# A prefix state in a causal linear-attention block: one fp32 product per chunk replaced by three fp32r products over halves, with the values stored twice

## The chip, the cores and the metric

The kernel runs on one NeuronCore of a Trainium2 chip. The metric is the device time of one execution in microseconds, taken as the median of several runs. The core's engines are named as in the profile: PE is TensorE's matmul, PEld its weight load, DVE is VectorE, ACT is ScalarE, POOL is GpSimd, and SP is SyncE, whose queue issues all of this kernel's DMA transfers.

## The reference

4096 tokens of width 512 go through a linear-attention layer with 16 query heads and 4 key/value heads of width 128, a layer norm, a gated feed-forward layer with Hadamard transforms, and another layer norm. The change lies in the attention, which is, for every head:

```python
q = q * cos + _rotate_half(q) * sin
k = k * cos + _rotate_half(k) * sin
qf = jax.nn.elu(q) + 1.0
kf = jax.nn.elu(k) + 1.0
def step(carry, inp):
    state, z = carry
    state = state + k_s[..., :, None] * v_s[..., None, :]
    z = z + k_s
    num = jnp.einsum('bhe,bhed->bhd', q_s, state)
    den = jnp.einsum('bhe,bhe->bh', q_s, z)[..., None] + EPS
    return ((state, z), num / den)
```

So a state of 128 by 128 (the sum of the outer products of k and v over all tokens so far) is carried along the sequence, and each token's query is multiplied with it.

## The kernel before

**Tiling.** The tokens are cut into 16 blocks of 256 (NB), each block into four chunks of 64. Two of the four key/value heads are done at a time: the loop `for i, (n, g, p) in enumerate(slots)` runs over n = 0 to 31 (the pass s = n // 16 over the head pair, the block b = n % 16), the head g of the pair and the half p of the block (two chunks). So a block has four slots, (0,0), (0,1), (1,0), (1,1), and there are 128 slots. In the first pass x is split into high and low halves and written to HBM (`xs_d`), in the second the halves are read back.

**Halves.** Most products are made in fp32r from operands that are split as hi = round(x) and lo = x - hi (`hilo`, L95 and L96): hi*hi + hi*lo + lo*hi, three matmuls accumulated in PSUM. The projections (`proj_v` L241, `proj` L288) are made so.

**What one block does.** `proj_v` makes v (ps_v, 128 tokens by 2 by 256), copies it in fp32 (v32, L245), makes its halves (vhl, high at L247 by ACT, low at L249 by DVE, each multiplied by rowm_s, which is zero at rows 0 and 64) and sends two sets of DMA copies from SBUF to SBUF: vd (each chunk's 64 rows stored twice, in partitions 0 to 63 and 64 to 127, four copies of 256 KB) and vs (v shifted by 63 rows, so that it lines up with the running sum that leads into a chunk, three copies). `rope` applies the rotary factors and elu + 1 (L268 to L278, over ACT, POOL and DVE). `proj_k` makes k (kft, transposed, L306 to L316 make its halves khl and the running sum z). `nat_k` transposes k back (pt, L325) and copies it to SBUF in fp32 (kfn, L327).

`state` adds a block's part to the running state for one head: four fp32 products of kfn and vs (L337), one per chunk, those of the even chunks over 64 rows and those of the odd chunks over 128:

```python
for i in range(4):
    r = slice(0, 64 * (i % 2) + 64)
    T.matmul(ps[:, i], B["kfn"][r, g, i // 2], B["vs"][r, i // 2, g * 128:(g + 1) * 128],
             start=True, stop=True)
```

Then DVE adds the state that came before (L348), ACT makes the high half sh (L353) and DVE the low half sl (L355). `scores` multiplies q with k inside a chunk (L380, L381), ACT and DVE fold the halves (L387, L390, L391) and POOL masks the result (A, L394). `av` adds state times q (sh and sl with qh and ql, three matmuls) and A times vd (two matmuls, L414), and the denominator (L415); ACT copies the result (num, L418), which goes to HBM by DMA.

**What sets the order.** The slot loop writes the calls in an order by hand: in slot (0,0) the state of block n for head 1, in (0,1) `proj_v` and `load_x` of later blocks, in (1,0) `nat_k` of block n + 1, in (1,1) the state of block n + 1 for head 0. Generators (`go`) split each call into pieces that are spread over a slot. q is projected five slots ahead (QA), the scores one (SA). Within that, a planner in the tile framework orders the instructions of each engine and of SP's queue by a simulated timeline; only those that the program pins (`pin`) keep their place. All DMAs go through SP, in order: a DMA that waits holds up those behind it.

**Buffers.** vs, vhl and kfn have one buffer, vd two, x1 three, num three, ds two; ps_s and pt share one PSUM bank (pst).

After the last slot come the output projection, layer norm, feed-forward stage and its output, which the change leaves as they are.

Of the kernel before, what the change touches and what calls it, by code (L numbers as in the profile page):

```python
# [9 lines left out]
F32 = mybir.dt.float32  # L10
# [33 lines left out]
def kernel(  # L44
# [3 lines left out]
    cs, ident, had, sel, rowm, out,  # L48
# [30 lines left out]
    rowm_s = cpool.tile([128, 1], F32, name="rowm_s")  # L79
# [8 lines left out]
    def load_raw(src):  # L88
        pool, tag = first.pop(0) if first else (praw, "raw")
        raw = pool.tile([128, 512], F32, tag=tag, name="raw")  # L90
        dma(raw, src)
        return raw
# [86 lines left out]
    with ExitStack() as es:  # L179
# [14 lines left out]
        G.memset(neg1, -1.0)  # L194
        W = {}
# [36 lines left out]
        def proj_v(n):  # L232
# [11 lines left out]
            v32 = pe.tile([128, 2, 256], F32, tag="v32", name="v32")  # L244
            S.activation(v32, ps, AF.Copy)  # L245
            vhl = p1.tile([128, 2, 2, 256], F32R, tag="vhl", name="vhl")
            S.activation(vhl[:, 0], ps, AF.Copy, scale=rowm_s)  # L247
            yield
            V.scalar_tensor_tensor(vhl[:, 1], ps, rowm_s, vhl[:, 0].bitcast(F32), ALU.mult, ALU.subtract)  # L249
            vd = p2.tile([128, 2, 4, 256], F32R, tag="vd", name="vd")  # L250
            for half in range(2):
                for par in range(2):
                    dst = vd[half * 64:half * 64 + 64].rearrange("p l (t r) d -> p l t r d", r=2)[:, :, :, par]
                    dma(dst, vhl[par * 64:par * 64 + 64])
            vs = p1.tile([128, 2, 256], F32, tag="vs", name="vs")
            dma(vs[63:128], v32[0:65])
            dma(vs[0:63, 1], v32[65:128, 0])
            if b:
                dma(vs[0:63, 0], blk[n - 1]["v32"][65:128, 1])
            else:  # L260
                G.memset(vs[0:63, 0], 0.0)
            B.update(v32=v32, vd=vd, vs=vs)

        def rope(ps, csb, f, stay=False):
# [8 lines left out]
            x1 = ps if stay else pe.tile([128, 2, 256], F32, tag="x1", name="x1", bufs=3)  # L273
# [45 lines left out]
        def nat_k(n):  # L319
# [6 lines left out]
            kfn = p1.tile([128, 2, 2, 128], F32, tag="kfn", name="kfn")  # L326
            S.activation(kfn, pt, AF.Copy)  # L327
            B["kfn"] = kfn
            B["S"] = []

        def state(n, g):
# [3 lines left out]
            for i in range(4):  # L335
                r = slice(0, 64 * (i % 2) + 64)
                T.matmul(ps[:, i], B["kfn"][r, g, i // 2], B["vs"][r, i // 2, g * 128:(g + 1) * 128],  # L337
                         start=True, stop=True)
# [16 lines left out]
            V.tensor_tensor(sl, s32, sh.bitcast(F32), ALU.subtract)  # L355
# [41 lines left out]
        def av(n, g, p):  # L397
# [10 lines left out]
            for c2 in range(2):  # L408
# [3 lines left out]
                       (B["vd"][:, 0, c, gs], A[:, c2]), (B["vd"][:, 1, c, gs], A[:, c2])]  # L412
# [4 lines left out]
            num = p3.tile([128, 4, 2, 64], F32, tag="num", name="num")  # L417
# [3 lines left out]
            if p == 1:  # L421
                ds = pout.tile([4, 256], F32, tag="ds", name="ds", bufs=2)
# [53 lines left out]
        first.extend([(praw, "raw")] * 3 + [(p3, t) for t in ("num", "s32", "sh", "sl") for _ in range(3)])  # L476
# [7 lines left out]
        dma(rowm_s, rowm)  # L484
# [27 lines left out]
        run(proj_v(0))  # L512
        weights_q(0, 0)
# [4 lines left out]
        nat_k(0)  # L518
# [15 lines left out]
        for i, (n, g, p) in enumerate(slots):  # L534
# [18 lines left out]
            if sl == (0, 0):  # L553
# [6 lines left out]
                gs2 = state(n, 1)  # L560
                go(gs2)
# [666 lines left out]
def _layout(inp):  # L1228
# [24 lines left out]
    for _ in range(7):  # L1253
# [3 lines left out]
    r = np.ones((128, 1), f)  # L1257
    r[0] = r[64] = 0
    arr["rowm"] = r
# [4 lines left out]
          "cs", "ident", "had", "sel", "rowm"]  # L1264
# [18 lines left out]
```

## Time and profile before

| what | value |
|---|---|
| median of 3 runs | 2303.36 us (2300.53 to 2303.75) |
| the profiled execution's own time | 2299.27 us |
| its span in the profile | 2297.6 us |
| attention stage (last state call) | from 0 to about 920 us |
| state products (L337), records and busy | 512, 112.3 us |
| mean granted PE clock | 0.994 |
| DMA, 50 to 900 us | 139.11 MB, mean 164 GB/s |

The page of a profile gives first the busy time of each engine. A busy time is the union of the records' lengths, and the matmuls' lengths overlap, since they are pipelined; the distance from one start to the next tells what one costs. A group of instructions is written as line, engine, operation, output and inputs, shapes, count. In the waits, what stands behind the arrow is what ended the wait. The timelines list start and length in us from the start of the span; merged lines have a count.

### The profile page before, as it was taken

What the parts mean: (1) busy time and instruction counts of PE and PEld (TensorE: products, weight loads), DVE (VectorE), ACT (ScalarE), POOL (GpSimd) and SP (SyncE); (2) the same over time, 40 slices, a digit from 0 to 9 for tenths busy, and PEclk for the clock granted to TensorE, in tenths of its full rate; (3) what the DMA queues carried; (4) which work ended last, traced back from release to release, by engine and by line L of the source; (5) the groups of instructions that cost most, each with busy time, mean ns of one, the idle gap of its engine ahead of it and who ended that gap; (6) DMA issues with size and microseconds to landing.
All of it is one profiled execution on the core that took longest, in us unless ns stands there. A gap on an engine that the chain in (4) does not pass through costs nothing. (4 is left out here: it accounts for less than half of the span.)

```text
span 2297.6 us, 42221 instructions
## 1 busy us (share of the span) xinstructions
PE 2258.7 (98%) x14432; PEld 2004.3 (87%) x14432; DVE 1757.2 (76%) x2684; ACT 1393.8 (61%) x2515; POOL 1280.1 (56%) x1063
## 2 busy tenths in 40 slices
PE   8999999999999999899999999999999999999998
PEld 7999999899999998688878878878788888899998
DVE  8888888888888878688898775766766766675555
ACT  7777777777777767444443466665555655464553
POOL 5556666555555545568797535665555555633332
PEclk9999999999999999999999999999999999999999
DMA  6665665555555544889998976876765757887773
GB/s 195 176 181 167 184 181 171 168 156 150 167 165 154 170 135 142 301 271 277 284 285 258 309 252 214 253 239 190 230 208 186 242 185 211 260 276 238 227 251 121
DMA packets 369527, 484.15 MB, mean 211 GB/s; under 512 B 68670, under 2 KB 224384, under 8 KB 365344
## 3 DMA queue, kind: packets, MB, share of 16 engines
q1 hardware_dynamic: 369312, 481.45, 68.4%
q8 instruction: 114, 1.87, 0.3%
q14 instruction: 101, 0.83, 0.1%
HBM read 282.76 MB, written 156.76 MB: 191 GB/s over the span
## 5 line engine op out<-in xcount | busy, mean ns | idle before, releaser
L288 PE MATMUL ps_qk<-xh,wh 128*128 128x256 f32 x1280 | 355.3, 278 | 0.0
L288 PE MATMUL ps_qk<-xl,wh 128*128 128x256 f32 x1280 | 354.9, 277 | 0.0
L288 PE MATMUL ps_qk<-xh,wl 128*128 128x256 f32 x1280 | 354.4, 277 | 0.0
L394 POOL TENSOR_SCALAR_AFFINE_SELECT A<-A 64x512 fp32r<-64x512 f32 x256 | 211.5, 826 | 241.8 <-DVE am L390 145.0
L1027 POOL TENSOR_TENSOR cc<-cc 128x512 f32<-128x512 f32 x96 | 149.0, 1554 | 288.8 <-ACT cc L1024 109.7
L96 DVE TENSOR_TENSOR wol<-A,woh 128x512 fp32r<-128x512 f32 x217 | 223.3, 1036 | 104.4 <-ACT woh L95 92.7
L270 POOL TENSOR_TENSOR sw<-sw,csb 128x512 f32<-128x512 f32 x160 | 208.5, 1303 | 135.2 <-ACT sw L269 124.2
L288 PEld LDWEIGHTS ps_qk<-xh,wh 128*128 128x128 f32 x1280 | 240.7, 188 | 3.0
L288 PEld LDWEIGHTS ps_qk<-xh,wl 128*128 128x128 f32 x1280 | 240.4, 188 | 0.9
L288 PEld LDWEIGHTS ps_qk<-xl,wh 128*128 128x128 f32 x1280 | 240.6, 188 | 0.3
L95 ACT ACTIVATE woh<-A 128x512 fp32r<-128x512 f32 x217 | 135.5, 630 | 134.6 <-PE ps_b L1045 76.5
L95 ACT ACTIVATE hah<-hraw 128x512 fp32r<-128x512 f32 x216 | 133.7, 629 | 125.5 <-PE ps_da L1196 63.8
L96 POOL TENSOR_TENSOR hal<-hraw,hah 128x512 fp32r<-128x512 f32 x78 | 106.9, 1374 | 175.2 <-PE ps_da L1196 75.0
L1045 PE MATMUL ps_a<-yoh,woh 128*128 128x512 f32 x512 | 202.6, 397 | 1.2 <-ACT sv L1052 1.0
L1045 PE MATMUL ps_a<-yol,woh 128*128 128x512 f32 x512 | 202.4, 395 | 0.0
L1045 PE MATMUL ps_a<-yoh,wol 128*128 128x512 f32 x512 | 199.8, 396 | 0.0
L96 DVE TENSOR_TENSOR hal<-hraw,hah 128x512 fp32r<-128x512 f32 x138 | 108.7, 796 | 98.0 <-PE ps_da L1196 40.0
L1052 ACT ACTIVATE sv<-ps_a,wsc 128x512 f32<-128x512 f32 x192 | 127.0, 680 | 38.1 <-PE ps_a L1045 37.8
L173 PE MATMUL ps_wo<-wh,oh 128*128 128x512 f32 x372 | 147.8, 397 | 2.1 <-ACT oh L95 2.1
L173 PE MATMUL ps_wo<-wh,ol 128*128 128x512 f32 x372 | 147.6, 397 | 0.0
L173 PE MATMUL ps_wo<-wl,oh 128*128 128x512 f32 x372 | 147.3, 396 | 0.0
L271 DVE TENSOR_TENSOR ps_qk<-ps_qk,csb 128x512 f32<-128x512 f32 x160 | 111.2, 695 | 32.6 <-ACT sw L269 30.9
(280 smaller groups left out, 7356.4 us busy)
## 6 DMA issues: line engine op xcount, KB each, us to landing
hraw<-hop_d SPq DMA_DIRECT2D x224, 256.0 KB
vd<-vhl SPq DMA_DIRECT2D x128, 256.0 KB
num_d<-num SPq DMA_DIRECT2D x128, 256.0 KB
rb<-rec_d SPq DMA_DIRECT2D x128, 256.0 KB
hop_d<-hS SPq DMA_DIRECT2D x128, 256.0 KB
nt<-num_d SPq DMA_DIRECT2D x31, 1024.0 KB
A<-in_wug_dram SPq DMA_DIRECT2D x93, 256.0 KB
hop_d<-cc SPq DMA_DIRECT2D x64, 256.0 KB
```

What stands on the lines that cost most here:

```text
L95: i = S.activation(hi, src, AF.Copy)
L96: j = eng.tensor_tensor(lo, src, hi.bitcast(F32), ALU.subtract)
L173: T.matmul(ps, l[:, h], r, start=i == 0, stop=i == 47)
L270: G.tensor_tensor(sw, sw, sinb, ALU.mult)
L271: V.tensor_tensor(ps, ps, cosb, ALU.mult)
L288: T.matmul(ps[:, j], W[key][wa][:, k * 128:(k + 1) * 128], B[xa][:, k], start=i == 0, stop=i == 11)
L394: G.affine_select(ah, ah.bitcast(F32), pattern=[[0, 8], [1, 64]], compare_op=ALU.is_ge, fill=0.0, base=0, channel_multiplier=-1)
L1027: G.tensor_tensor(x, x, c.pop(("g", q)), ALU.mult)
L1045: T.matmul(ps, w[:, u, k], y[:, k], start=first and i == 0, stop=i == 5, skip_group_check=not first)
L1052: S.activation(x, ps, AF.Copy, scale=sc)
```

## The change

The state's products are made in fp32r from halves. k's transposed-back copy is split into high and low (kfn gets a dimension of two, the low half by DVE from PSUM). v's copy for the state, vst, holds both halves, and holds v for both chunks of a pair side by side in 256 columns: the even chunk's columns are zero in partitions 64 to 127, so that both chunks take the same 128 rows of k, and one product serves two chunks. Per call that is two pairs times three products of 256 columns. The zeros are written once, as vst has one buffer; the fp32 copy v32 is gone. The last 63 rows of a block's halves are kept in vcar for the next block. The halves lie side by side in vhl, vst and vd, so that the copies have rows of 2 KB, and vst's copies are issued ahead of vd's. vd becomes two fixed tiles VD whose rows 0 and 64 are zeroed once, and its copies leave out these rows (63 rows in place of 64); rowm, which zeroed them, is gone with its input and its load. The low half of the state of head 1 goes to GpSimd. x1, num and ds lose a buffer each. `nat_k` becomes a generator, and the very last `state` call moves from slot (0,0) of the last block to slot (1,1) of the block before.

Left out of the diff are only the lines that take away rowm's tile, input and load.

```diff
@@ -86,8 +85,8 @@
         tc.keep_in_program_order(i)
 
     def load_raw(src):
-        pool, tag = first.pop(0) if first else (praw, "raw")
-        raw = pool.tile([128, 512], F32, tag=tag, name="raw")
+        pool, tag, nb = first.pop(0) if first else (praw, "raw", 3)
+        raw = pool.tile([128, 512], F32, tag=tag, name="raw", bufs=nb)
         dma(raw, src)
         return raw
@@ -192,6 +191,22 @@
         G.memset(ones4, 1.0)
         neg1 = p1.tile([128, 1], F32, name="neg1")
         G.memset(neg1, -1.0)
+        vst = pe.tile([128, 2, 2, 2, 256], F32R, name="vst", bufs=1)
+        vcar = pe.tile([128, 2, 256], F32R, name="vcar", bufs=1)
+        VD = [p2.tile([128, 4, 2, 256], F32R, tag="vd", name="vd") for _ in range(2)]
+
+        def zero(eng, dst):
+            src = ones4[0:dst.shape[0], 0:1, None].to_broadcast(list(dst.shape))
+            if eng is S:
+                S.activation(dst, src, AF.Copy, scale=0.0)
+            else:
+                V.tensor_scalar(dst, src, 0.0, None, ALU.mult)
+
+        for l in range(2):
+            for k in range(2):
+                zero(S if k else V, VD[k][:, 2 * l:2 * l + 2].rearrange("p c l d -> p (c l) d"))
+            zero(V, vst[64:128, l, 0])
+            zero(S, vst[0:64, 0, l])
         W = {}
         blk = {}
@@ -241,25 +256,28 @@
                         T.matmul(ps[:, t], B[xa][:, k, t * 128:(t + 1) * 128], w[:, k % 2],
                                  start=i == 0, stop=i == 11)
                         i += 1
-            v32 = pe.tile([128, 2, 256], F32, tag="v32", name="v32")
-            S.activation(v32, ps, AF.Copy)
-            vhl = p1.tile([128, 2, 2, 256], F32R, tag="vhl", name="vhl")
-            S.activation(vhl[:, 0], ps, AF.Copy, scale=rowm_s)
-            yield
-            V.scalar_tensor_tensor(vhl[:, 1], ps, rowm_s, vhl[:, 0].bitcast(F32), ALU.mult, ALU.subtract)
-            vd = p2.tile([128, 2, 4, 256], F32R, tag="vd", name="vd")
+            vhl = pe.tile([128, 2, 2, 256], F32R, tag="vhl", name="vhl", bufs=1)
+            S.activation(vhl[:, :, 0], ps, AF.Copy)
+            yield
+            V.tensor_tensor(vhl[:, :, 1], ps, vhl[:, :, 0].bitcast(F32), ALU.subtract)
+            dma(vst[63:128, :, 1], vhl[0:65])
+            dma(vst[63:64, :, 0], vhl[0:1])
+            dma(vst[0:63, 1], vhl[65:128, 0, None].to_broadcast([63, 2, 2, 256]))
+            if b:
+                dma(vst[0:63, 0], vcar[0:63, None].to_broadcast([63, 2, 2, 256]))
+            vd = VD[n % 2]
             for half in range(2):
                 for par in range(2):
-                    dst = vd[half * 64:half * 64 + 64].rearrange("p l (t r) d -> p l t r d", r=2)[:, :, :, par]
-                    dma(dst, vhl[par * 64:par * 64 + 64])
-            vs = p1.tile([128, 2, 256], F32, tag="vs", name="vs")
-            dma(vs[63:128], v32[0:65])
-            dma(vs[0:63, 1], v32[65:128, 0])
-            if b:
-                dma(vs[0:63, 0], blk[n - 1]["v32"][65:128, 1])
-            else:
-                G.memset(vs[0:63, 0], 0.0)
-            B.update(v32=v32, vd=vd, vs=vs)
+                    dst = vd[half * 64 + 1:half * 64 + 64].rearrange("p (t r) l d -> p t r l d", r=2)[:, :, par]
+                    dma(dst, vhl[par * 64 + 1:par * 64 + 64])
+            if b == 0 and n:
+                zero(V, vst[0:63, 0, 0])
+                zero(V, vst[0:63, 0, 1])
+            B.update(vhl=vhl, vd=vd)
+
+        def carry(n):
+            if n < N and n % NB < NB - 1:
+                dma(vcar[0:63], blk[n]["vhl"][65:128, 1])
 
         def rope(ps, csb, f, stay=False):
             cosb = csb[:, 0:1].to_broadcast([128, 2, 256])
@@ -270,7 +288,7 @@
             G.tensor_tensor(sw, sw, sinb, ALU.mult)
             V.tensor_tensor(ps, ps, cosb, ALU.mult)
             yield
-            x1 = ps if stay else pe.tile([128, 2, 256], F32, tag="x1", name="x1", bufs=3)
+            x1 = ps if stay else pe.tile([128, 2, 256], F32, tag="x1", name="x1", bufs=2)
             V.scalar_tensor_tensor(x1, ps, 1.0, sw, ALU.add, ALU.add)
             S.activation(sw, x1, AF.Exp, bias=neg1)
             yield
@@ -323,19 +341,21 @@
             for g in range(2):
                 for j in range(2):
                     T.transpose(pt[:, g, j], kft[:, g, 1 + 128 * j:129 + 128 * j], idt)
-            kfn = p1.tile([128, 2, 2, 128], F32, tag="kfn", name="kfn")
-            S.activation(kfn, pt, AF.Copy)
+            kfn = pe.tile([128, 2, 2, 2, 128], F32R, tag="kfn", name="kfn", bufs=1)
+            S.activation(kfn[:, 0], pt, AF.Copy)
             B["kfn"] = kfn
             B["S"] = []
+            yield
+            V.tensor_tensor(kfn[:, 1], pt, kfn[:, 0].bitcast(F32), ALU.subtract)
 
         def state(n, g):
             s, b = divmod(n, NB)
             B = blk[n]
             ps = pst.tile([128, 4, 128], F32, tag="st", name="ps_s")
-            for i in range(4):
-                r = slice(0, 64 * (i % 2) + 64)
-                T.matmul(ps[:, i], B["kfn"][r, g, i // 2], B["vs"][r, i // 2, g * 128:(g + 1) * 128],
-                         start=True, stop=True)
+            for j in range(2):
+                for i, (k, v) in enumerate(((0, 0), (0, 1), (1, 0))):
+                    T.matmul(ps[:, 2 * j:2 * j + 2], B["kfn"][:, k, g, j], vst[:, j, :, v, g * 128:(g + 1) * 128],
+                             start=i == 0, stop=i == 2)
             s32 = p3.tile([128, 4, 128], F32, tag="s32", name="s32")
             for i in (0, 2):
                 if i:
@@ -352,7 +372,7 @@
             yield
             S.activation(sh, s32, AF.Copy)
             yield
-            V.tensor_tensor(sl, s32, sh.bitcast(F32), ALU.subtract)
+            (G if g else V).tensor_tensor(sl, s32, sh.bitcast(F32), ALU.subtract)
 
         def proj_q(j):
             n, g, hp = j // 4, j // 2 % 2, j % 2
@@ -409,17 +429,17 @@
                 c = 2 * p + c2
                 t = slice(64 * c, 64 * c + 64)
                 ops = [(sh[:, c], qh[:, :, t]), (sh[:, c], ql[:, :, t]), (sl[:, c], qh[:, :, t]),
-                       (B["vd"][:, 0, c, gs], A[:, c2]), (B["vd"][:, 1, c, gs], A[:, c2])]
+                       (B["vd"][:, c, 0, gs], A[:, c2]), (B["vd"][:, c, 1, gs], A[:, c2])]
                 for i, (l, r) in enumerate(ops):
                     T.matmul(ps[:, c2], l, r, start=i == 0, stop=i == len(ops) - 1)
                 T.matmul(den, selr[:, c], A[:, c2], start=c == 0, stop=c == 3)
             gg = 2 * s + g
-            num = p3.tile([128, 4, 2, 64], F32, tag="num", name="num")
+            num = p3.tile([128, 4, 2, 64], F32, tag="num", name="num", bufs=2)
             S.activation(num.rearrange("p h c q -> p c h q"),
                          ps.rearrange("p c (h q) -> p c h q", h=4), AF.Copy)
             dma(num_d[2 * b + p][:, gg], num.rearrange("p h c q -> p (h c q)"))
             if p == 1:
-                ds = pout.tile([4, 256], F32, tag="ds", name="ds", bufs=2)
+                ds = pout.tile([4, 256], F32, tag="ds", name="ds", bufs=1)
                 S.activation(ds, den, AF.Copy, bias=EPS_DEN)
                 for j in range(2):
                     dma(den_d[2 * b + j][gg].rearrange("h c q -> c h q"),
@@ -473,7 +493,7 @@
         N = 2 * NB
         slots = [(n, g, p) for n in range(N) for g in range(2) for p in range(2)]
         NQ = len(slots)
-        first.extend([(praw, "raw")] * 3 + [(p3, t) for t in ("num", "s32", "sh", "sl") for _ in range(3)])
+        first.extend([(praw, "raw", 3)] * 3 + [(p3, "num", 2)] * 2 + [(p3, t, 3) for t in ("s32", "sh", "sl") for _ in range(3)])
 
         def early_raw(key, src):
             RAW0[key] = load_raw(src)
@@ -510,12 +529,13 @@
                 pass
 
         run(proj_v(0))
+        carry(0)
         weights_q(0, 0)
         run(proj_k(0))
         run(proj_q(0))
         weights_q(0, 1)
         run(proj_q(1))
-        nat_k(0)
+        run(nat_k(0))
         run(load_x(1))
         for j in range(2):
             c = slice(j * 512, (j + 1) * 512)
@@ -557,8 +577,9 @@
                     gv = proj_v(n + 1)
                     go(gv)
                 go(gs1)
-                gs2 = state(n, 1)
-                go(gs2)
+                if nxt:
+                    gs2 = state(n, 1)
+                    go(gs2)
             elif sl == (0, 1):
                 if n < N - 2:
                     gv = proj_v(n + 1)
@@ -568,7 +589,9 @@
                     run(load_x(n + 2))
             elif sl == (1, 0):
                 if nxt:
-                    nat_k(n + 1)
+                    gn = nat_k(n + 1)
+                    go(gn)
+                    carry(n + 1)
             else:
                 gs1 = state(n + 1, 0) if nxt else None
                 go(gs1)
@@ -585,8 +608,14 @@
                     go(gv)
             elif sl == (0, 1):
                 go(gv)
+            elif sl == (1, 0):
+                if nxt:
+                    go(gn)
             elif sl == (1, 1):
                 go(gs1)
+                if n == N - 2:
+                    gs2 = state(N - 1, 1)
+                    go(gs2)
             av(n, g, p)
             if sl == (0, 0):
                 go(gs2)
```

More of the change, by code (lines that the diff above doesn't have):

```diff
@@ L47 @@
     x_t, x_n, wq, wk, wv, wo, su_ug, su_dp, ws_ug, ws_dp, wug, wd,
-    cs, ident, had, sel, rowm, out,
+    cs, ident, had, sel, out,
 ):
@@ L78 @@
     idt = cpool.tile([128, 128], F32, name="idt")
-    rowm_s = cpool.tile([128, 1], F32, name="rowm_s")
     selr = cpool.tile([128, 4, 4], F32R, name="selr")
@@ L483 @@
             early_raw(("v", 0, j), wv[0, :, j * 512:(j + 1) * 512])
-        dma(rowm_s, rowm)
         for j in range(2):
@@ L1256, in _layout @@
     arr["sel"] = c(np.tile(np.eye(4, dtype=f).reshape(1, 16), (128, 1)))
-    r = np.ones((128, 1), f)
-    r[0] = r[64] = 0
-    arr["rowm"] = r
     return arr
 _ORDER = ["x_t", "x_n", "wq", "wk", "wv", "wo", "su_ug", "su_dp", "ws_ug", "ws_dp", "wug", "wd",
-          "cs", "ident", "had", "sel", "rowm"]
+          "cs", "ident", "had", "sel"]
 def kernel(**inputs):
```

## The prediction

> **What bounds the kernel now.** I read the page first, then a table by stretch, then the engines' timelines within one block, then the waits. The page names the engine:
>
> ```profile
> span 2297.6 us, 42221 instructions
> PE 2258.7 (98%) x14432; PEld 2004.3 (87%) x14432; DVE 1757.2 (76%) x2684; ACT 1393.8 (61%) x2515; POOL 1280.1 (56%) x1063
> PEclk9999999999999999999999999999999999999999
> ```
>
> TensorE is busy 98% of the span at full clock. The change touches only the first stage, about 0 to 922 us, so I cut two pairs of blocks out of it, one from the first pass over the blocks (s=0) and one from the second (s=1). Columns: stretch, its length, busy us and instructions of PE, PEld, DVE, ACT, POOL, clock, DMA share, GB/s.
>
> ```profile
> 316.80:344.30 27.50, 27.50 (x225) 26.06 (x224) 24.59 (x40) 20.74 (x40) 15.63 (x16) 1.00 0.65 192
> 344.30:372.90 28.60, 28.60 (x234) 27.13 (x233) 25.55 (x40) 21.39 (x40) 17.81 (x18) 1.00 0.58 167
> 544.50:572.50 28.00, 28.00 (x229) 26.55 (x229) 23.82 (x40) 20.39 (x38) 14.86 (x16) 1.00 0.56 152
> 572.50:600.50 28.00, 28.00 (x229) 26.59 (x228) 24.07 (x39) 19.87 (x37) 14.28 (x15) 1.00 0.62 177
> ```
>
> A block takes 28.0 us in both passes and PE is never idle in it. So what PE is spared comes off the span until another engine is late. VectorE is next: 25.1 of 28.05 us in the first pass, 23.95 of 28.0 in the second. The waits agree: between 50 and 880 us PE's matmuls waited for others 5.5 us in all (four rows), and not once for the state's operands.
>
> The work that changes, in PE's timeline (start, length, line, shape, count):
>
> ```profile
> 400.93 0.28 PE L288 MATMUL ps_qk<-xh,wh 128*128 128x256 f32 x1
> 401.05 0.28 PE L288 MATMUL ps_qk<-xl,wh 128*128 128x256 f32 x1
> 401.26 1.74 PE L337 MATMUL ps_s<-vs,kfn 64*128 64x128 f32 x8
> 402.75 0.36 PE L288 MATMUL ps_qk<-xh,wl 128*128 128x256 f32 x1
> ...
> 405.19 0.28 PE L414 MATMUL ps_num<-qh,sh 128*128 128x256 f32 x1
> 405.31 0.28 PE L414 MATMUL ps_num<-ql,sh 128*128 128x256 f32 x1
> 405.43 0.28 PE L414 MATMUL ps_num<-qh,sl 128*128 128x256 f32 x1
> ```
>
> The lengths overlap; the cost is the distance of starts. A 256-column fp32r product costs 0.12 us. The eight records of one state call (four fp32 products, two records each) hold PE from 401.05 to 402.75, 1.70 us, of which 0.12 is the matmul before: 1.58 us.
>
> **The products.** Removed: 64 calls x 1.58 = 101 us. Added: 64 calls x 6 products of 128x128 weights and 256 columns, whose nearest row is L414's qh,sh: 6 x 0.12 = 0.72, 46 us. Net 0.86 per call, 1.72 per block, 55 us. A block's floor on PE is 28.0 - 1.72 = 26.3 us.
>
> Here a rule speaks against the change. The Trainium skill, "FP8 and Floating Point Precision", section TensorE Precision Notes, gives true fp32 four passes through the array. A pass of 128 columns at the rate of the row above is 0.06 us, so four passes are 0.24 per product and 0.94 per call; against 0.72 the change would spare 0.22 per call, 14 us. The trace has 1.58, almost twice that, so I take the trace; the 14 us are a rival's number.
>
> **VectorE, ScalarE, GpSimd.** DVE gains the low half of k from PSUM, 0.69 (row: ql from ps_qk, 686 ns), and loses the sl of the odd group, 0.89 (L355, 888 ns); the low half of v stays one instruction (0.75 before, about 0.69 after). Per block -0.25. ACT loses the v32 copy, 0.60. POOL gains the sl, 1.30 (row: sw, 1303 ns), 16 to 18 of 26.3 us; it is due one or two slots later, so it is hidden unless it delays the masking of A. DVE then has 24.8 us of work in 26.3 in the first pass and 23.7 in the second, 94% and 90%, in order, with waits for ACT and PE between. Its idle time shrinks from 3.0 and 4.0 us per block to 1.5 and 2.6. Two bounds for what that costs: nothing (the waits that go are slack), or, if 1 us more of the present idle time can't be pressed out, about 1 us per block, 30 us. I take 0.45 in the first pass and 0.2 in the second: 10 us.
>
> **Transfers.** Before, per block: four vd copies (1 MB, 1 KB rows) and three vs copies (0.26 MB). After: four vd copies of 63 rows in 2 KB runs, three or four vst copies and one vcar copy, some 0.9 MB. About 950 runs of 2 KB in place of about 1150 of 1 KB and 65 of 2 KB; by packet records of this stage 1 KB took 69 ns and 2 KB 100 ns on average, so engine time is 5.9 us per block in place of 5.4, beside a DMA share of 0.56 to 0.65. Volume is no bound. What counts is when the state's operand lands. The issues now, SP's timeline:
>
> ```profile
> 555.30 0.82 SPq L58 DMA_DIRECT2D vs<-v  x1
> ...
> 564.77 1.62 SPq L58 DMA_DIRECT2D vs<-v  x2
> 566.50 3.38 SPq L58 DMA_DIRECT2D vd<-vhl  x4
> 569.98 0.95 SPq L58 DMA_DIRECT2D num_d<-num  x1
> ```
>
> and the engines' side:
>
> ```profile
> 564.15 0.60 ACT L245 ACTIVATE v<-ps_v 128x512 f32<-128x512 f32 x1 [1.69 <-PE ps_v L241]
> ...
> 565.57 0.75 DVE L249 SCALAR_TENSOR_TENSOR vhl<-ps_v,rowm_s,vhl 128x512 fp32r<-128x512 f32 x1
> ...
> 572.50 1.74 PE L337 MATMUL ps_s<-vs,kfn 64*128 64x128 f32 x8
> ```
>
> vs needs only ACT's copy and leaves at 564.8. vst needs DVE's low half too, done at 566.3. Then SP issues 65 rows (0.85), one row (0.4), 63 rows (0.85): until 568.5. By the semaphore updates in the trace, the 63-row vs copy issued at 565.67 landed at 567.96, 2.3 us later; with four times its bytes (1.4 us of packets per engine in place of 0.5) about 3.2. Landing about 570.9, state at 572.5: 1.6 us to spare where there were 4.5. The piece from the block before (vcar) can go early, as the vs piece at 555.30 does. I take 0.1 us per block, 3 us; bounds 0 and the second rival. The 63 rows matter: the Trainium skill, "DMA: Bandwidth & Descriptors", section on why a semaphore goes up by 16, says that a copy uses the largest number of engines up to 16 that divides its rows, 9 for 63. The trace's updates agree (9 for the 63-row vs copy, 13 for 65 rows, 16 for a 64-row vd copy). vd then has 4 x 14 runs on each of nine engines, 5.6 us, landing near 576; its first reader is at 584. num_d, queued behind vd on SP, may land near 577, where ACT writes that buffer again (two buffers for three): 0 to 1 us in one slot of four, of which I take nothing, as ACT idles 8 us per block (behind a waiting num copy stand ACT's sw copies, on which POOL's and DVE's rotary products wait). The vcar copy waits on SP for the vst piece that reads it; num_d stands behind it, with the same cover. Low half of k: DVE between 569.8 and 572.5, one product's wait at most, in the same 3 us.
>
> **Fewer buffers, start and end.** x1 (2 for 3) and ds (1 for 2) are read within a few us and rewritten 6 to 13 us later: nothing; if that cover went, about 0.7 us of an in-order engine per use. The zeroing adds four instructions each to ACT and DVE, 1.0 us for 1024 columns by the 0.59 of 512, 0.6 for the small ones: 3.2 us on each, while ACT has its first data at 3.52 and DVE at 4.18. Outside bounds 0 and 2 us; I take 1. Moving the last state call forward by a slot: -1 to +1, zero. The later stages keep their work and move forward as a whole.
>
> **Sum.** 55 - 10 - 3 - 1 = 41 us. Against the profiled execution: 2299.27 (span 2297.6 and 1.7 around it) - 41 = 2258. The runs' median stands 4.1 us above that execution, so 2303.4 - 41 = 2262.
>
> **Rivals.**
> 1. DVE becomes the bound: period about 27.1 us instead of 26.3, 31 x 0.9 = 28 us gained, 2275. For it: 94% in order, and POOL's sl slows DVE instructions with SBUF operands (sl itself 0.67 to 1.14). Against: PE never waited for it, and the slots are 7 us long. Chance 0.24.
> 2. The other side: vst lands late and PE stands at the first state call of every block, all behind it in order. It decides when landing slips more than 1.6 + 1.72 us, past about 574.2. If SP puts the four vd copies (3.4 us of issue) or num_d and den_d ahead of vst, landing is near 575 and later; a stall of 2.5 us per block costs 31 x (2.5 - 1.72) = 24, giving 2327. For it: the spare is thin, nine engines carry all the copies. Against: vst stands first in the program. Chance 0.15. A smaller stall of about 1 us, 2290: chance 0.08.
> 3. The change spares less than it says, 14 us by the four-pass rule: 2289 before losses. Only if the fp32 records hide other waiting; but the 1.70 recurs in nearly every call. Chance 0.05, half of it within 0.2%.
>
> **Numbers.** Likeliest case 0.48, 2246 (all of 55 and a little at the end) to 2270. Range 2246 to 2292, which takes in rival 1 and the small stall and leaves out rival 2 and some of 3. Faster by over 0.2% (4.6 us, about what a measurement of this kernel can tell from no change) 0.81, within 0.03, slower 0.16.
>
> **What would show it.** State calls of six records in 0.72 us at a block period of 26.3 to 26.7; DVE above 90% in the stretches; a PE wait at the state call for vst or for the low k not above 0.3 us. A period of 27 with PE waits for A, ql or sl is rival 1; a PE gap before ps_s ended by a DMA is rival 2; state products at over 0.2 us each would break the sum itself.

## The result and the profile after

The kernel after takes 2314.38 us (median of 5 runs, 2310.42 to 2322.2) where the kernel before, beside it, takes 2300.7 (2299.88 to 2303.75). The ratio is 1.0061, with a 95% interval of 1.0037 to 1.0085. It is 0.6% slower; the prediction was 2262, faster.

The page of the kernel after, against the three lines shown of before:

```profile
span 2317.6 us, 42125 instructions
...
PE 2234.5 (96%) x14304; PEld 2009.6 (87%) x14304; DVE 1740.6 (75%) x2690; ACT 1377.5 (59%) x2487; POOL 1303.4 (56%) x1093
...
PEclk9999999899999999899999999999999999999999
```

PE's busy time fell by 24 us, yet the span grew by 20: PE now stands still for 83 us, before for 39. Two of the 40 slices have a PE clock below 0.9: that from 406 to 463 us, at the change of passes, and that from 927 to 985 us, where the later stages begin. The table by stretch shows the two passes; its first row lies in the first pass, its second in the second. The columns are those of the prediction's table (PE, PEld, DVE, ACT, POOL, clock, DMA share, GB/s). Kernel before:

```profile
130.00:350.00 220.00, 220.00 (x1793) 208.83 (x1794) 196.53 (x308) 164.90 (x307) 132.88 (x128) 1.00 0.61 177
470.00:860.00 390.00, 390.00 (x3175) 369.90 (x3176) 332.85 (x537) 279.44 (x514) 201.40 (x211) 1.00 0.55 154
```

and the kernel after:

```profile
130.00:350.00 220.00, 218.66 (x1842) 215.30 (x1841) 200.66 (x323) 168.59 (x314) 148.48 (x144) 1.00 0.66 210
470.00:860.00 390.00, 368.28 (x2978) 358.12 (x2977) 317.43 (x519) 262.09 (x482) 199.80 (x217) 0.97 0.57 171
```

In the first pass the forecast came true: PE is never idle for long, and more instructions go through in the same 220 us on every engine. In the second pass PE is idle 22 of 390 us, its mean clock is 0.97, and PEld, DVE and ACT do less in the same time than before. Volume is no reason: the DMA share moved from 0.55 to 0.57.

By the starts of PE's denominator products (ps_den), eight per block, the span splits as follows, in us:

| from, to | before | after | difference | predicted |
|---|---|---|---|---|
| start to first block's av | 42.8 | 44.0 | +1.2 | +1 |
| block 0 to 1 | 32.5 | 33.9 | +1.4 | not split off |
| blocks 1 to 12, 11 periods | 308.4 | 294.6 | -13.8 | 11 x (-1.72 + 0.45 + 0.1) = -12.9 |
| blocks 12 to 17, change of passes | 144.4 | 156.5 | +12.0 | about -6 to -7 |
| blocks 17 to 29, 12 periods | 336.4 | 353.8 | +17.4 | 12 x (-1.72 + 0.2 + 0.1) = -17.0 |
| block 29 to the last av | 68.6 | 66.2 | -2.4 | about -3 |
| later stages | 1364.4 | 1368.7 | +4.3 | 0 |

In blocks 1 to 12 and 17 to 29 the periods are 28.0 to 28.1 before; after, they lie between 26.3 and 27.3 in the first pass, and run from 27.3 to 32.8 in the second. So two of seven rows explain the result: the second pass, 34 us off, and the change of passes, some 18 off.

The products are as predicted. PE's timeline of the kernel after (one of the six records is missing):

```profile
614.81 0.28 PE L306 MATMUL ps_qk<-xh,wl 128*128 128x256 f32 x1
614.93 0.76 PE L357 MATMUL ps_s<-vst,kfn 128*128 128x256 f32 x5
615.53 0.28 PE L400 MATMUL ps_sc<-qh,khl 128*128 128x256 f32 x1
```

From 614.93 to 615.53 five products start, 0.12 each; with all six recorded, the distance is 0.71.

**What PE waits for.** First the waits of ACT between 50 and 880 us, then those of PE (total us, times, longest):

```profile
ACT num L438 <- DMA num_d<-num: 41.7, 15, 4.4
...
ACT wh L94 <- DMA raw<-in_wv_dram: 4.4, 1, 4.4
```

```profile
PE ps_sc L400 <- DVE A L411: 16.8, 13, 6.5
PE ps_v L256 <- DVE ql L388: 7.7, 7, 4.9
PE ps_num L434 <- ACT sh L373: 7.4, 6, 2.5
...
PE ps_s L357 <- DMA vst<-vhl: 0.8, 4, 0.3
```

PE doesn't wait for vst, which was the second rival. It waits for A, ql and sh, results of DVE and ACT. And ACT, in front of them, waits 41.7 us for its own output buffer: num can't be written again until its DMA to HBM has read it. 39.1 of these 41.7 us lie after 465 us. Before, this wait does not occur between 50 and 880 us. How it comes about shows in one block of the second pass. SP's queue, kernel after:

```profile
600.94 2.53 SPq L58 DMA_DIRECT2D vst<-vhl  x3
603.51 4.47 SPq L58 DMA_DIRECT2D vd<-vhl  x4
608.08 1.73 SPq L58 DMA_DIRECT2D num_d<-num  x1
609.91 1.45 SPq L58 DMA_DIRECT2D den_d<-ds  x2
```

ACT in the same block:

```profile
600.13 0.58 ACT L438 ACTIVATE num<-ps_num 128x512 f32<-128x512 f32 x1
...
604.40 0.58 ACT L438 ACTIVATE num<-ps_num 128x512 f32<-128x512 f32 x1
...
609.60 0.58 ACT L407 ACTIVATE A<-ps_sc 64x512 fp32r<-64x512 f32 x1
614.10 0.60 ACT L438 ACTIVATE num<-ps_num 128x512 f32<-128x512 f32 x1 [3.92 <-DMA num_d<-num]
...
614.86 0.71 ACT L293 ACTIVATE sw<-x,neg 128x512 f32<-128x512 f32 x1
```

The num written at 600.13 is ready at 600.7, but seven copies stand ahead of its DMA on SP. It is issued at 608.08 and landed at 614.01 (the last of its 16 semaphore updates in the trace), 13.9 us after the write began. With two buffers the next write but one needs that tile, at about 610.2. ACT stands 3.92 us, and its exp at 614.86 is late, and with it the rotary products and A. Kernel before, ACT:

```profile
565.93 0.59 ACT L418 ACTIVATE num<-ps_num 128x512 f32<-128x512 f32 x1
...
576.97 0.60 ACT L418 ACTIVATE num<-ps_num 128x512 f32<-128x512 f32 x1 [0.18 <-PE ps_num L414]
```

Here the num written at 565.93 was issued at 569.98 (the prediction shows the line) and landed at 575.10, 9.2 us; the next write but one came at 576.97, and there were three buffers. This block is one of the slow ones of before: in 9 of 14 blocks between 470 and 860 us num_d of this slot left ahead of the vd copies, and landed 3.5 to 4.3 us after its write. In the kernel after, all 13 have seven or six copies in front, and by the median 7.9 us pass from the write to the issue and 6.1 from there to the landing, 14.1 in all, against a next write but one at 11.0. In the first pass of the kernel after SP's order is the same, but the next write but one comes 13.1 us after the first (301.42 and 314.51), not 10.1; there the wait adds up to 1.0 us.

Then PE, some us later:

```profile
621.64 0.39 PE L434 MATMUL ps_num<-qh,sh 128*128 128x256 f32 x1 [0.87 <-ACT sh L373]
...
623.22 0.51 PE L400 MATMUL ps_sc<-qh,khl 128*128 128x256 f32 x1 [1.08 <-DVE A L411]
...
624.38 0.41 PE L256 MATMUL ps_v<-wh,xh 128*128 128x256 f32 x1
624.60 0.41 PE L256 MATMUL ps_v<-wl,xh 128*128 128x256 f32 x1
```

The distance of starts is 0.22, not 0.12: after idling about 1.95 us in 2.5 PE runs at half clock, for 3.4 us until 626.7. By the clock record such windows take 10.2 us of clock between 465 and 860 us, and another 10.2 between 360 and 465; before, none. The second of these stretches, before and then after:

```profile
360.00:465.00 105.00, 102.12 (x821) 96.03 (x820) 91.75 (x148) 80.02 (x149) 61.28 (x61) 1.00 0.60 170
360.00:465.00 105.00, 91.04 (x701) 88.69 (x700) 81.71 (x133) 69.20 (x128) 57.14 (x57) 0.90 0.55 170
```

The Trainium skill, "TensorE: Matmul & The Clock Gate", Part 1, describes a gate that watches windows of about 3.4 us and halves the clock after an idle one. The length agrees; but here PE was still at work for a fifth of those 2.5 us, so less than a whole idle window suffices. In this trace half clock sets in only at steps of 3.41 us. Between 60 and 900 us it does so eight times, each time after a step in which PE, by its records, was at work for 0 to 53% of the time; of the steps at full clock without that sequel the least busy had 51, 59 and 60%. So about half a step of idle time was enough here.

At the change of passes another wait begins the loss. ACT, then PE:

```profile
373.64 0.63 ACT L94 ACTIVATE wh<-raw 128x512 fp32r<-128x512 f32 x1 [4.42 <-DMA raw<-in_wv_dram]
```

```profile
379.10 0.58 PE L256 MATMUL ps_v<-wh,xh 128*128 128x256 f32 x1 [4.86 <-DVE ql L388]
```

The weights of v for the second pass are issued at 369.1 and land at 373.6; ACT waits for them in order, PE stands 4.86 us a little later, and then comes the half clock.

### The profile page after: what moved, and what is told of

It reads as the page before. It is cut to its first block, busy times and chain, and to the rows that moved or that the text cites. A ratio compares the mean times of both kernels' runs of the same rounds, so it can differ in the third digit from the quotient of the medians.

```text
span 2317.6 us, 42125 instructions
## 1 busy us (share of the span) xinstructions
PE 2234.5 (96%) x14304; PEld 2009.6 (87%) x14304; DVE 1740.6 (75%) x2690; ACT 1377.5 (59%) x2487; POOL 1303.4 (56%) x1093
## 5 line engine op out<-in xcount | busy, mean ns | idle before, releaser
L306 PE MATMUL ps_qk<-xh,wh 128*128 128x256 f32 x1280 | 361.2, 282 | 0.1
L306 PE MATMUL ps_qk<-xl,wh 128*128 128x256 f32 x1280 | 360.4, 282 | 0.0
L306 PE MATMUL ps_qk<-xh,wl 128*128 128x256 f32 x1280 | 359.8, 281 | 0.0
L414 POOL TENSOR_SCALAR_AFFINE_SELECT A<-A 64x512 fp32r<-64x512 f32 x256 | 191.5, 748 | 148.5 <-DVE am L410 97.1
```

The costliest lines, as they stand in the source:

```text
L306: T.matmul(ps[:, j], W[key][wa][:, k * 128:(k + 1) * 128], B[xa][:, k], start=i == 0, stop=i == 11)
L414: G.affine_select(ah, ah.bitcast(F32), pattern=[[0, 8], [1, 64]], compare_op=ALU.is_ge, fill=0.0, base=0, channel_multiplier=-1)
```

## The experiments

Two theories. **Place and buffers**: num_d (and den_d) go out late since they stand behind vst and vd on SP, and num and ds have one buffer less. **Engines**: the copies of 63 rows use nine DMA engines, so all that stands behind them lands late. A third stays from the prediction: **DVE**, 94% busy in order. "Before" beside the runs is 2299 to 2302 us; ratios are to it. The second-pass period is the mean from block 17 to 29. In the diffs "..." marks lines left out.

### Buffers and rows, each alone

e1: num back to three buffers (room made by am).

```diff
-am = p2.tile([64, 512], F32, tag="am", name="am")
+am = p2.tile([64, 512], F32, tag="am", name="am", bufs=1)
-num = p3.tile([128, 4, 2, 64], F32, tag="num", name="num", bufs=2)
+num = p3.tile([128, 4, 2, 64], F32, tag="num", name="num", bufs=3)
...
```

> The changed kernel with three num buffers again (am has one buffer in place of two to make room; am is written and read by DVE alone). Theory N (in the second pass ACT waits about 2.8 us per block to overwrite a num buffer whose copy to HBM has not landed, and everything in order behind it is late): the ACT wait for num_d, 41.7 us between 50 and 880 us, falls under 8 us, the period of the second pass from 29.3 to 26.3 to 27.0 us, the time to 2262 to 2275. Theory R (the queue of nine DMA engines itself delays what PE needs): the wait moves elsewhere, period 28 or more, time 2290 to 2310. Theory D (VectorE and the planner's order set the period): time within 10 us of 2312.

Measured: 2307.25, ratio 1.0029 (1.0016 to 1.0042), second-pass period 28.99. The num wait went, and another took its place:

```profile
ACT ds L443 <- DMA den_d<-ds: 36.4, 16, 3.4
```

The den_d copies stand behind the same seven issues, and ds has one buffer. So a buffer for one of two outputs behind the same issues leaves the other's wait.

e2: vd copies of 64 rows, 16 engines. The zeros in rows 0 and 64 of vd are left out (v stands there), so this kernel, like e3 and e8, serves for the time alone.

```diff
-dst = vd[half * 64 + 1:half * 64 + 64].rearrange("p (t r) l d -> p t r l d", r=2)[:, :, par]
-dma(dst, vhl[par * 64 + 1:par * 64 + 64])
+dst = vd[half * 64:half * 64 + 64].rearrange("p (t r) l d -> p t r l d", r=2)[:, :, par]
+dma(dst, vhl[par * 64:par * 64 + 64])
```

> The changed kernel with vd copies of 64 rows in place of 63 (the two zero rows of vd are overwritten by v, so this part of the computation is changed), which use 16 engines in place of 9. Theory N with R as its cause: num_d lands 2 to 3 us earlier, the ACT wait for it falls from 41.7 to under 15 us, the second pass to about 27 us per block, time 2265 to 2280. Theory N without R (only the buffer count matters): the wait stays above 30 us, time within 10 us of 2312. Theory D: within 10 us of 2312.

Measured: 2287.59, 0.9948 (0.9931 to 0.9964), second pass 27.93. All engines and SP have the same instructions in the same order as in the kernel after, so the 27 us come from the rows of the vd copies alone. By the medians of the second pass the four vd issues take 3.4 us of SP in place of 4.5, and num_d, issued 1.0 us sooner after its write, still takes 5.9 us to land (6.1 in the kernel after). ACT's wait falls by half, and a wait for vst appears. ACT's line and PE's:

```profile
ACT num L438 <- DMA num_d<-num: 19.6, 13, 1.9
```

```profile
PE ps_s L357 <- DMA vst<-vhl: 11.0, 13, 1.4
```

e3: both edits.

> Both: three num buffers (one am buffer) and 64-row vd copies (vd's zero rows are overwritten, so this part of the computation is changed). Theory N: not more than 6 us better than three num buffers alone, 2258 to 2272. Theory R: clearly better than either alone. Theory D: still above 2300.

Measured: 2287.39, 0.995 (0.9935 to 0.9965), second pass 27.70: no more than e2 alone. The num wait is gone, but 13.5 us of den_d's wait stand in its place.

e4: the kernel before with two num buffers.

```diff
-num = p3.tile([128, 4, 2, 64], F32, tag="num", name="num")
+num = p3.tile([128, 4, 2, 64], F32, tag="num", name="num", bufs=2)
...
```

> The kernel before with two num buffers and nothing else changed. If the missing buffer alone makes the loss: an ACT wait for num_d appears in the second pass and the time rises by 20 us or more, above 2320. If it needs the nine-engine vd copies or the shorter period beside it (theory N with R): num_d of before landed at about 574.6 for a reuse at 577.0, so no wait above 5 us in all, time within 6 us of 2301.

Measured: 2308.14, 1.0038 (1.0023 to 1.0053). There is no num wait, and the periods stay at 28.0; of the 10.1 us of its profile 2.3 come before the last av and 7.8 in the later stages, which the edit does not touch. So two buffers alone cost the attention's periods nothing in the order of before. Most of the 7.8 us, and of the +4.3 of the table above, goes with half clock: over the later stages it takes 5.6 us of clock before, 9.2 in the kernel after and 11.2 in e4. Of this, 5.1 (after) and 6.8 (e4) fall in the first 60 us behind the last av, where before has none. What brings it on there was not tested. (The landing at 574.6 in the expectation is the last but one of 16 updates; the last came at 575.10.)

### All buffers, all engines, and a way round vcar

e5: num 3, ds 2, am 1, and vcar gone (its rows go straight from vhl to vst). e6: that, and every copy of 63 rows cut into 48 + 15, the one of 65 into 64 + 1.

```diff
-dma(vcar[0:63], blk[n]["vhl"][65:128, 1])
+dma(vst[0:63, 0], blk[n]["vhl"][65:128, 1, None].to_broadcast([63, 2, 2, 256]))
...
```

and, for e6, of its cuts the one of vd:

```diff
-dma(dst, vhl[par * 64 + 1:par * 64 + 64])
+for lo, hi in ((0, 48), (48, 63)):
+    dma(dst[lo:hi], vhl[par * 64 + 1 + lo:par * 64 + 1 + hi])
...
```

> The changed kernel with both output buffers restored, num 3 and ds 2; room comes from am with one buffer and from vcar, which is gone (the last 63 rows go from vhl to vst directly, after the state call of head 1). The copies stay on nine engines. Theory N widened (ACT waits for whichever output buffer is short, because its copy is queued behind vd): ACT's waits for num_d and den_d, 41.7 and in the first experiment 36.4 us, both fall under 8 us, second pass 27.0 to 27.8 us per block, time 2278 to 2292. Theory R (nine engines): the wait moves to another reader, above all PE's wait for vst, second pass above 28.3, time above 2295.

> As the run with both buffers restored, and every copy of 63 rows cut into one of 48 and one of 15 rows, the copy of 65 rows into one of 64 and one-row copies, so that 16 and 15 engines work on them: some six issues more on SP per block. Theory R: second pass 0.5 us per block or more under the run with the buffers alone, time 2270 to 2284. If SP's issue time counts more than the engines: slower than that run, above 2292. If the buffers were all of it: within 5 us of that run.

Measured: e5 2284.16, 0.993 (0.9912 to 0.9948), second pass 26.79, change of passes +8.8 against before. e6 **2262.01** (2260.89 to 2265.81), 0.9832 (0.9817 to 0.9846), second pass 26.40 in every block, change of passes -7.9. The stretch of e6 beside those above:

```profile
470.00:860.00 390.00, 389.42 (x3300) 384.88 (x3298) 354.09 (x571) 287.88 (x528) 227.10 (x240) 1.00 0.67 187
```

PE is busy throughout and DVE 91%, so DVE at that load does not set the period; the third theory falls. e6 is faster than both kernels, at the time that was forecast for the kernel after. The exact figure is in part luck: by the rows of the table above the forecast is off by up to 3 us, some up, some down.

e7: e6 with the first of the v weights loaded two slots earlier, against the wait at the change of passes.

```diff
+if r == -8:
+    RAW0["v", 1, 0] = load_raw(wv[1, :, 0:512])
```

> As the run with buffers and wide copies, and the first piece of the second pass's weights for v is loaded two slots earlier, since in the changed kernel ACT stood 4.4 us for it at the change of passes and PE 4.9 us after it. If that wait is the loss at the change of passes (the five blocks from n=12 take about 20 us more than five of the first pass, before 4): 8 to 12 us less than the run without it, 2262 to 2276. If the loss there is the work of the weights' conversion itself: within 4 us.

Measured: 2268.46, 0.9856 (0.9841 to 0.987). The expectation was wrong: the wait for v's weights (2.1 us in e6) went, but ACT waits 3.9 us for the weights of q (2.0 in e6), and the change of passes takes 142.2, not 136.5. The planner also ordered the engines anew there.

e8: e3 with the low half of head 1's state back on DVE.

```diff
-(G if g else V).tensor_tensor(sl, s32, sh.bitcast(F32), ALU.subtract)
+V.tensor_tensor(sl, s32, sh.bitcast(F32), ALU.subtract)
```

> As the run with three num buffers and 64-row vd copies (vd's zero rows are overwritten, so this part of the computation is changed), and the low half of the state of head 1 back on VectorE. If GpSimd's longer work and its hold on VectorE's operands cost time in the second pass: 5 to 15 us under that run's 2287. If VectorE is what limits: 5 us or more above it, first pass above 27.0 us per block. If neither is near a limit: within 4 us of 2287.

Measured: 2292.31, 0.9966 (0.9953 to 0.9979), against e3's 2287.39: the first pass at 27.06 in place of 26.76, the second faster (27.31 for 27.70). But the last av comes at 918.0 in e8 and at 917.8 in e3; the difference lies in the later stages, which the edit leaves alone. The planner also ordered every engine anew (some 430 of ACT's 2487 instructions moved), and num_d went ahead of vd in the second pass. So what moving sl to POOL is worth is not shown.

### Buffers and engines crossed

e9 is the kernel after without vcar and with am 1, num and ds still short; e10 is that with the cut copies.

> The fourth corner's control: the changed kernel with vcar gone (rows go straight to vst) and am with one buffer, but num 2 and ds 1 as in the change, copies on nine engines. If those two side edits of the runs with restored buffers do nothing: within 8 us of 2314, an ACT wait for num_d of 30 us or more. If the direct copy was what helped there: near 2285.

> The same with the copies cut so that 16 and 15 engines work on them, output buffers still short (num 2, ds 1). If the nine engines are the whole cause and the short buffers only show it: within 5 us of 2262, second pass under 26.7 us per block. If buffers and engines add up (each hides a part): 2275 to 2295, ACT's waits for num_d or den_d 10 to 25 us in all. If only the buffers count: above 2300.

Measured: e9 2318.76, 1.008 (1.0063 to 1.0097); e10 2303.71, 1.0011 (1.0002 to 1.0019). With e5 and e6, in us:

| | 63 rows in one copy | cut copies |
|---|---|---|
| num 2, ds 1 | 2318.8 (e9) | 2303.7 (e10) |
| num 3, ds 2 | 2284.2 (e5) | 2262.0 (e6) |

Buffers are worth 35 and 42 us, engines 15 and 22. Along the columns the order of the instructions hardly differs. Along the rows the planner also ordered the stretch from 350 to 550 us anew, and 9.9 and 16.7 us of the gain lie there (blocks 12 to 17), so that part is not the engines' alone. ACT's wait in e10, and one block of its SP queue:

```profile
ACT num L439 <- DMA num_d<-num: 44.2, 16, 4.3
```

```profile
613.76 3.73 SPq L58 DMA_DIRECT2D vst<-vhl  x5
617.54 6.21 SPq L58 DMA_DIRECT2D vd<-vhl  x8
623.86 0.48 SPq L58 DMA_DIRECT2D num_d<-num  x1
```

The wait is as long as in the kernel after (41.7). More engines did shorten the landing, from 6.1 us after the issue to 2.7 (medians of the second pass), but thirteen issues in place of seven hold num_d on SP for 11.1 us after its write in place of 7.9, so it lands 13.8 us after it, as late as before the cut. So e10 does not clear the engines; it shows that both parts count, and that both come from the copies put ahead. The rest of the study tests that place.

### The place on the queue

e11: num_d and den_d issued by ACT's own queue; e12: the same in e6.

```diff
-dma(num_d[2 * b + p][:, gg], num.rearrange("p h c q -> p (h c q)"))
+nc.scalar.dma_start(num_d[2 * b + p][:, gg], num.rearrange("p h c q -> p (h c q)"))
...
```

> The changed kernel as it is (num 2, ds 1, vcar, nine engines), but num_d and den_d are issued by ACT right after the copy that fills the buffer, on ACT's own DMA queue, so that they don't stand behind vst and vd on SP. If the 7 us that num_d stands on SP behind vst and vd are the cause: ACT's waits for num_d and den_d fall from 42 to under 8 us, second pass 26.4 to 27.3 us per block, time 2265 to 2285 (the loss at the change of passes stays). If the backlog of the DMA engines is the cause, whichever queue issues: the waits stay above 25 us, time above 2300.

> The best version so far (both buffers restored, copies on 16 and 15 engines, 2262) with num_d and den_d issued by ACT. Its second pass is at PE's floor of 26.4 us already, so if only waits of output buffers are at stake: within 5 us of 2262. If ACT's issue time shows: up to 10 us more.

Measured: e11 2371.83, 1.0313 (1.0283 to 1.0343); e12 2333.98, 1.0148 (1.0127 to 1.0168). Inconclusive: the buffer wait is gone, but the planner, given other costs, orders every engine anew (some 750 of ACT's 2487 instructions moved in e11), ACT now stands 78 us for DMAs, most of them other copies' (53 in the kernel after), and in e11 PE waits for ACT's num copy:

```profile
PE ps_num L434 <- ACT num L438: 35.7, 16, 5.7
```

So e13 changes only SP's order: num_d and den_d of slot (0,1) go ahead of the four vd copies, both pinned; buffers, rows and engines stay as in the kernel after, and PE, DVE, ACT and POOL keep its order instruction by instruction. e14 does it in e10.

```diff
+        def vd_copies(n, pinned=False):
...
+                    dma(dst, vhl[par * 64 + 1:par * 64 + 64], pinned)
...
-            dma(num_d[2 * b + p][:, gg], num.rearrange("p h c q -> p (h c q)"))
+            dma(num_d[2 * b + p][:, gg], num.rearrange("p h c q -> p (h c q)"), (g, p) == (0, 1))
...
             av(n, g, p)
...
+            if sl == (0, 1):
+                vd_copies(n + 1, True)
```

> The changed kernel with one thing moved: on SP's queue the copies num_d and den_d of slot (0,1) stand ahead of the four vd copies of the next block in place of behind them. The order of PE, DVE, ACT and POOL is the same, and so are buffers and the nine engines. If the place on SP behind vd is what makes num_d late: ACT's wait for num_d falls from 42 to under 10 us, second pass 26.4 to 27.3 us per block, time 2270 to 2288 (the loss at the change of passes stays). If the backlog of the engines behind the vst copies is enough: the wait stays above 25 us, time above 2300.

> The same move in the kernel with short output buffers and copies on 16 and 15 engines, which took 2304 with a second pass of 28.9. If the place on the queue is the whole cost of the short buffers: second pass 26.4 to 26.8, time 2260 to 2270, as with the buffers restored. If the buffers hide more than that: 2275 or more.

Measured: e13 2280.17, 0.9917 (0.9902 to 0.9932); e14 2268.08, 0.9865 (0.9849 to 0.9882). SP's queue in e13:

```profile
587.88 2.51 SPq L58 DMA_DIRECT2D vst<-vhl  x3
590.50 0.42 SPq L58 DMA_DIRECT2D num_d<-num  x1
591.02 1.72 SPq L58 DMA_DIRECT2D den_d<-ds  x2
592.80 4.01 SPq L58 DMA_DIRECT2D vd<-vhl  x4
```

and its second pass:

```profile
470.00:860.00 390.00, 386.49 (x3260) 381.89 (x3260) 346.59 (x567) 287.09 (x527) 224.47 (x238) 1.00 0.62 186
```

num_d leaves at 590.50 instead of some 4 us later and lands at 594.78, 7.7 us after its write; the num wait is gone, and of the half clock one window of 3.4 us is left between 465 and 860 us. The move takes num_d out from behind vd on SP and, after the issue, on the DMA engines; which of the two counts for more it does not tell. Most second-pass blocks take 26.4 to 26.5, with two buffers for num, one for ds and nine engines; from block 17 to 29 it is 320.9, 33 less than after. Moving four issues down the queue gave back 34 us. e14 lands some 6 us above e6 without e6's buffers. In the profiles it is 8.1, of which 5.7 lie in the later stages (1370.9 against 1365.2): once the place is right, the short buffers cost the attention some 2 us at most. The change of passes is still +8.2 in e13 (ACT's wait for the v weights is 5.2 us there) and -4.9 in e14, which has the cut copies, but also lacks vcar and has one buffer for am.

## Why the prediction was wrong

**Products: right.** 0.72 per call was predicted, 0.71 measured, and every kernel in which nothing else stands (e6, e14) has periods of 26.4. Four passes at the rate of an fp32r pass would have given 27.6 at best; that reading is refuted here.

**DVE: right in size.** 0.45 for the first pass and 0.2 for the second were taken; with 0.1 for vst the forecast was 26.85 and 26.6, and e6 has 26.75 and 26.40. The first rival (27.1 throughout) did not occur. Whether DVE makes the 0.45 is not shown: PE's records leave only 1.3 us idle in 220 of the first pass. One reading was too strong: "PE never waited for it", where DVE's A had ended three of PE's waits before, 2.2 us in all. By the prediction's signs PE's waits for A and ql would speak for this rival; here they came from ACT's stall, since in e13, with DVE's order kept, PE no longer waits for DVE in the second pass. POOL's sl ended PE waits of 0.7 us, so it was hidden; whether it was needed, e8 does not tell.

**vst: right in the kernel after** (0.8 us of waits in all). So the second rival, which had the sign right, named the wrong wait. It did show, 10 to 11 us, in e2 and e3, whose blocks are shorter, but not in e13; the reason is not shown.

**num_d: this step failed.** This is the step that turned the forecast gain into a loss. The prediction had the buffer, the seven issues ahead of it, the landing near 577 by before's clock and ACT's next write, and valued it at "0 to 1 us in one slot of four, of which I take nothing, as ACT idles 8 us per block". Two things were wrong with it. The size: num_d landed 13.9 us after the write, where the prediction's own 577 is 11.1 after 565.93, in part since the vd issues took 4.47 us for 3.38 and num_d's own 1.73 for 0.95; and ACT's next write came 10.1 us after the first, where before it was 11.0. "One slot of four" was right, but the row it was read from was no measure of the kernel before, whose num_d mostly went ahead of vd. The stall was 3 to 4 us, not 0 to 1. And the cover: ACT's 8 idle us per block are no reserve, since they are waits for PE and DVE spread over the block. ACT works in order, and a stall of 3 us ahead of an exp reached DVE, POOL and PE inside one block. The parenthesis even named who stands behind it. 39.1 us in 13 waits are 3.0 per block of the second pass, and e13 gave back 32.9 over 12 blocks, 2.7 each: nearly all of the stall had reached the end, the half clock included.

**ds: also failed.** "Read within a few us and rewritten 6 to 13 us later: nothing" left out that den_d stands behind the same issues; e1 shows 36.4 us of it as soon as num no longer hides it.

**The change of passes: not in the prediction.** It was counted as ordinary blocks. In the kernel after it begins with ACT's wait for the v weights. From the kernel after to e2, which differ in the rows of the vd copies alone and have one order, blocks 12 to 17 fall from 156.5 to 146.8 us: 9.7 of the 12 us that were lost there go with the copies of 63 rows. The pairs with cut copies agree in sign (16.7 from e5 to e6, 9.9 from e9 to e10), but the planner's order differs there too. Which copy holds what up is not shown, and e7 moved the load of the weights without gain. That stays open.

**Nine engines: named, but not priced beyond vst.** The Trainium skill, "DMA: Bandwidth & Descriptors", section on why a semaphore goes up by 16, gives by its rule 9 engines for 63 rows and 16 for 48. The updates in the runs' traces agree (9, and 16 for a 48-row copy of e10). The prediction used it for landing times only; the 64-row copies of e2 gave 27 us and the cut copies 15 to 22.

## What to carry to other kernels

When copies are put first on an in-order DMA queue, list every output copy behind them, and set its landing against the next write of its buffer, with the shorter period that the change itself brings. Idle time of an in-order engine is no cover for a stall in it unless that stall falls into one of its waits. Cut a copy with an awkward row count into parts that use all engines, but count the issues that this adds ahead of others: in e10 they took back on SP what the engines gave. Move the issues before buying buffers: here four issues moved were worth 34 us.

## What the runs showed of the hardware

- A DMA issue on SP is not constant: num_d of slot (0,1) took 0.42 us behind three copies (e13) and 1.73 behind seven (after); four vd copies took 3.38 before (64 rows) and 4.47 after (63).
- An fp32 product of 128 columns held PE 0.40 us (1.58 for four), an fp32r product of 256 columns 0.12.
- About 1.95 us of idle PE in 2.5 us was followed by 3.4 us at half clock, so the price of such a wait nearly doubled: 1.7 us on top. In the kernel after every such window between 60 and 900 us followed 3.4 us in which PE was at work for 53% or less.
